# Two adaLN layers on one core: batch 0's feed-forward norm and gate stage put into layer 1's timetable, and weight loads and folds given other times

## The chip, the cores and the metric

One core of a Trainium2 chip runs the whole program. The metric is device microseconds per execution. Engines have their names of the profile: PE is the matmul engine (PEld its weight loads), DVE, ACT and POOL the three others that compute, SP the one that only issues DMAs. POOL issues DMAs too. Each engine works through its own queue in order.

## What is computed

x has 8 batches of 512 tokens by 256 features. Two layers of the same frame follow each other:

```python
def layer(x, c, wmod):
    sa, ca, ga, sb, cb, gb = silu(c) @ wmod          # per batch
    x = x + ga * attention(layernorm(x) * (1 + ca) + sa)
    return x + gb * ffn(layernorm(x) * (1 + cb) + sb)

# layer 1
def attention(h):        # 16 heads of 16, rotary q and k, causal softmax
    q, k, v = rope(h @ wq), rope(h @ wk), h @ wv
    return softmax(causal(q @ k.T / 4)) @ v @ w_proj + b_proj

def ffn(h):              # w1, w2: 256 -> 1024; h1, h2: 1024 -> 1024; w3: 1024 -> 256
    g = silu(h @ w1.T * s1) * (h @ w2.T * s2)
    g = gelu(g @ h1.T * s3)
    g = gelu(g @ h2.T * s4)
    return g @ w3.T * s5
```

Layer 0 has linear attention beside a sliding window of 64, and another feed-forward; the change hardly touches it. The weights w1, w2, h1, h2 and w3 hold -1, 0 and 1.

## The kernel before

**One timetable for three quarters of the work.** All of layer 0 and layer 1's attention are written as small closures, each with a due time, and sorted by it into one order; no scheduler moves them. `when(time, f)` books layer 0, which takes 20 units of time per batch; `when1(time, f)` books layer 1, with 24 units per batch, counted from layer 1's start. Layer 1 starts while the last batch of layer 0 is still at work, so that the two share a stretch (their seam). `in_time` is the one or the other. A closure issues the instructions of one small step (one bank of matmuls, one activation), and each engine's queue is what the sorted order leaves on it.

**Layer 1's attention.** `prepare1(b)` (L939) gets a batch ready. `fetch` loads its rows of `x_mid` (layer 0's result in DRAM). `normed` (L296 and after) books four statistics on DVE (`st`, `mv`), one root on ACT and DVE, and four normalizing activations on ACT. `by_features` transposes the rows on PE, eight 128x128 transposes for a batch, and `modulated` (L993) moves each bank out of PSUM by an ACT activation that applies scale and shift; `hT` is its result. `rotation` makes the q and k of a half of the heads: two matmuls (L1070 among them), an ACT copy (`k`, L1034) and the rotary products on DVE and POOL; the last of its times, in `apart`, are copies. `fold` (L966 to L977) multiplies the projection's weights by the batch's gate row, so that the residual costs nothing later: part 0 fetches the row `bc` on SP, part 1 is two POOL products (L973 the first, into `wps`), parts 2 and 3 two POOL sums. Then, in 6 units for 4 heads, come the scores (L1102, L1160), the exponentials (L1171 on ACT), the causal mask (L1175 on POOL) and the values (L1194). `kept_sums1` (L1204) copies the sums `ys` on ACT, `by_tokens1` (L1210) transposes them, `normalized1` (L1220, L1221) divides on DVE, and `project_out` (L1239 to L1264) transposes into `aT`, projects, and stores to `x_mid`.

**The feed-forward's weights and its flag.** `bring(4)` (L870 to L900), booked at layer 1's unit 48.2, closes layer 0's pools and loads, on SP, the projection's weights `wproj` and `bproj`, and on POOL (L894) w1T, w2T and w3T, 1 MB each. `look` and `low_bits` (L912 to L923) bring every weight once more and reduce its low 12 bits to a column of `low`; `looked` (L928 to L933) reduces `low` to one flag. If no weight has low bits set, products of the weights with a number that is split into two parts, `hi` (cast to fp32r) and `lo` (the rest), are exact enough, and the feed-forward runs in fp32r, two matmuls for each product. Else a plain fp32 version runs. The flag is loaded into a register by all engines (L1451), and a branch follows.

**The feed-forward** (L1321 and after) is ordered by the framework's own scheduler, after the timetable has ended. It opens its own pools, and issues the loads of h1 and h2 on POOL, 512 KB apiece, eight for each (L1337). `layernorm` (L142 to L147) and `transposed` (L157) prepare batch 0. Then for each batch come stage 1 (w1 and w2, `sg` by Silu on ACT L1413, the product `row` on DVE L1414, the two parts by `split` L1341 and L1342), the h1 stage and the h2 stage (L1370 the matmuls, Gelu L1419 and L1425), and w3 with the residual (L1436, L1444, L1445) and the store L1446. Each PSUM bank holds a product of 128 features by 512 tokens; in exact mode `times` makes one by 2 x 2 matmuls in stage 1 (L1370), by 8 x 2 in the h1 and h2 stages.

These two lines of the branch are the seam between timetable and feed-forward:

```python
inexact = nc.values_load(full["flag"][0:1, 0:1], min_val=0, max_val=1)
with tc.If(inexact < 1) as whole:
```

Of the kernel before, what the change touches and what calls it, by code (L numbers as in the profile page):

```python
# [17 lines left out]
P = 128  # L18
# [17 lines left out]
def adaln_two_layers_kernel(ctx: ExitStack, tc: tile.TileContext, t, out):  # L36
# [149 lines left out]
    def mod_rows(pool, b, first, n, bufs=2):  # L186

        bc = pool.tile([P, n, D], FP, name="bc", tag="bc", bufs=bufs)
        nc.sync.dma_start(out=bc, in_=mod_dram[b, first : first + n, :].partition_broadcast(P))
        return bc  # L190

    with ExitStack() as lctx:
# [481 lines left out]
        def finish(b):  # L677
# [45 lines left out]
            for j, ats_ in ((0, (34.6, 34.95)), (2, (35.45, 35.85))):  # L723
# [7 lines left out]
                [t0 + i for i in (35.6, 35.8, 36.28, 36.29)],  # L731
                t0 + 36.5,
                [t0 + 37.4 + 0.15 * j for j in range(NTB)],
                "hr",
# [125 lines left out]
        def bring(i):  # L860
# [7 lines left out]
            elif i == 2:  # L868


                cmask = got1["cmask"] = fm.tile([P, T], FP, name="cmask", tag="cat0", bufs=2)
                nc.gpsimd.memset(cmask, 0.0)
                diag = cmask[:, T - P : T]
                nc.gpsimd.affine_select(
                    out=diag, in_=diag, pattern=[[-1, P]], compare_op=ALU.is_ge, fill=-4e9, base=0, channel_multiplier=1
                )
            elif i == 3:

                home = [rp.tile([P, 2, T], FP, name="home", tag="aw", bufs=4) for _ in range(2)]
                got1["wproj"], wps[0] = (home[0][:, i, :].rearrange("p (k n) -> p k n", k=NC) for i in range(2))  # L880
                got1["bproj"], got1["bc"] = (home[1][:, 0, i * D : (i + 1) * D] for i in range(2))
                nc.sync.dma_start(out=got1["wproj"], in_=w_proj)
                nc.sync.dma_start(out=got1["bproj"], in_=t["L1_attn_b_proj"].partition_broadcast(P))
                nc.sync.dma_start(out=got1["bc"], in_=mod_dram[0, 4, :].partition_broadcast(P))
            else:
                only0.close()
                fpool = ctx.enter_context(tc.tile_pool(name="ffn_w", bufs=1, side="right"))
                lp = got1["lp"] = only1.enter_context(tc.tile_pool(name="only1", bufs=1, side="right"))
                got1["wproj"] = load(lp, "wproj", [P, NC, D], w_proj)
                got1["bproj"] = load(lp, "bproj", [P, D], t["L1_attn_b_proj"].partition_broadcast(P))  # L890

                for name, n, cols in (("w1T", NC, DH), ("w2T", NC, DH), ("w3T", NF, D)):
                    dst = full[name] = fpool.tile([P, n, cols], FR, name=name, tag=name)
                    nc.gpsimd.dma_start(out=dst, in_=t[name].rearrange("(k p) n -> p k n", p=P))  # L894
                for name in ("w1_s_cols", "w2_s_cols", "h1_s_cols", "h2_s_cols"):
                    full[name] = load(fpool, name, [P, NF], t[name])
                full["w3_s"] = load(fpool, "w3_s", [P, D], t["L1_ffn_w3_s"].partition_broadcast(P))
                full["x0"] = fpool.tile([P, NTB, D], FP, name="x0", tag="x0")
                full["low"] = fpool.tile([P, 22], FP, name="low", tag="low")
                full["flag"] = fpool.tile([1, 1], I32, name="flag", tag="flag")  # L900
# [3 lines left out]
        for i, at in enumerate((146.2, 150.0, 157.0, 171.5)):  # L904
            when(at, lambda i=i: bring(i))
        when1(48.2, lambda: bring(4))


# [30 lines left out]
        def prepare1(b):  # L939
# [7 lines left out]

            early = ((135.5, (138.7, 0.3), 139.75, (142.15, 0.4)), (153.0, (160.6, 1.0), 164.6, (165.2, 0.3)))
            usual = (t0 - 37.0, (t0 - 33.6, 1.0), t0 - 29.4, (t0 - 28.6, 0.6))
# [16 lines left out]
            def fold(i):  # L966
                if i == 0:
                    held["bc"] = mod_rows(got1["lp"], b, 4, 1, 1)[:, 0, :] if b else got1["bc"]
                    if b:
                        wps[b] = got1["lp"].tile([P, NC, D], FP, name="wps", tag="wps", bufs=2)  # L970
                elif i == 1:
# [6 lines left out]

            at = (31.0, 49.0)[b] if b < 2 else t0 + 6.5
            for i in range(4):  # L980
                when1(at + (0.0, 3.0, 4.0, 5.0)[i], lambda i=i: fold(i))

# [18 lines left out]
            for c, at in enumerate(((148.38, 149.4), (166.45, 168.9), (t0 - 24.55, t0 - 18.55))[min(b, 2)]):  # L1001
                in_time(at, lambda c=c: by_features(c))
                in_time(at + (0.12 if b == 0 else 0.45), lambda c=c: modulated(c))

# [47 lines left out]
            for c, which, at, begin, then, turn, last in (  # L1052
                (0, "k", -11.55, 152.50, 153.0, (153.3, 153.6, 154.2, 154.8), (156.0, 156.3)),
                (0, "q", -8.55, 153.50, 154.1, (155.0, 155.4, 156.0, 156.6), (157.9, 158.2)),
                (1, "k", 0.45, 156.70, 157.2, (157.5, 158.0, 158.6, 159.2), (160.3, 160.8)),
                (1, "q", 3.45, 157.70, 158.3, (159.9, 160.2, 160.8, 161.4), (162.2, 162.7)),
            ):
# [254 lines left out]
        when1(24 * 3, lambda: nc.gpsimd.dma_start(out=full["x0"], in_=x_mid[0].rearrange("(j p) d -> p j d", p=P)))  # L1312
        when1(24 * B + 2, looked)
        tc.keep_in_program_order(nc.scalar.preload_act_table_set("natural_log_exp_and_others"))
        with tc.manual_schedule():
            for _, _, what in sorted(plan, key=lambda p: p[:2]):
                what()
        only1.close()


    def feed_forward(exact):  # L1321

        with ExitStack() as fctx:
            hp = fctx.enter_context(tc.tile_pool(name=f"hw{exact}", bufs=1 if exact else 3))
            gp = fctx.enter_context(tc.tile_pool(name=f"g2{exact}", bufs=2))
            tok = fctx.enter_context(tc.tile_pool(name=f"tok2{exact}", bufs=1))
            mm = fctx.enter_context(tc.tile_pool(name=f"mm2{exact}", bufs=8, space=PSUM))

            if exact:
                h1 = hp.tile([P, NF, DH], FR, name="h1", tag="h1")
                h2 = hp.tile([P, NF, DH], FR, name="h2", tag="h2")
                for dst, name in ((h1, "h1T"), (h2, "h2T")):
                    src = t[name].rearrange("(k p) n -> p k n", p=P)
                    for k in range(NF):
                        nc.gpsimd.dma_start(out=dst[:, k, :], in_=src[:, k, :])  # L1337
                full.update(h1T=h1, h2T=h2)

            def split(hi, lo, src):  # L1340
                nc.vector.tensor_copy(hi, src)  # L1341
                nc.vector.tensor_tensor(lo, src, hi.bitcast(FP), ALU.subtract)  # L1342

            def halves(name, pool, n):

                if not exact:
                    whole = pool.tile([P, n, T], FP, name=name, tag=name[0])
                    return [whole], lambda k: whole[:, k, :], lambda k: None
                parts = [pool.tile([P, n, T], FR, name=name + e, tag=name[0] + e) for e in "hl"]
                held = {}  # L1350

                def row(k):
                    held[k] = tok.tile([P, T], FP, name="row", tag="row", bufs=3)
                    return held[k]

                return parts, row, lambda k: split(parts[0][:, k, :], parts[1][:, k, :], held.pop(k))

# [20 lines left out]

            if exact:
                w3s = full["w3T"]  # L1380
            else:
                w3s = load(hp, "w3g", [P, NF, D], t["w3T"].rearrange("(k p) n -> p k n", p=P))

            xs, hs = {0: full["x0"]}, {}

            def first_product(b, xn):

                hs[b], row, done = halves("hT", tok, NC)

# [7 lines left out]

            first_product(0, layernorm(tok, xs[0], 1))
            for b in range(B):
                x = xs.pop(b)  # L1400
                if b + 1 < B:
                    xs[b + 1] = tok.tile([P, NTB, D], FP, name="x", tag="x", bufs=2)
                    nc.sync.dma_start(out=xs[b + 1], in_=x_mid[b + 1].rearrange("(j p) d -> p j d", p=P))
                bc = mod_rows(tok, b, 5, 1, 1)
                gb = bc[:, 0, :]
                nc.vector.tensor_tensor(gb, gb, full["w3_s"], ALU.mult)  # L1406
                h = hs.pop(b)
                g1, row, done = halves("g1", gp, NF)
                for f in range(NF):
                    pa = times("w1T", NC, f * P, h)  # L1410
# [4 lines left out]
                    done(f)  # L1415
                g2, row, done = halves("g2", gp, NF)
                for f in range(NF):
                    ps = times("h1T", NF, f * P, g1)
                    nc.scalar.activation(row(f), ps, AF.Gelu, scale=full["h1_s_cols"][:, f : f + 1])  # L1419
                    done(f)  # L1420
                xn = layernorm(tok, xs[b + 1], 1) if b + 1 < B else None
                g3, row, done = halves("g3", gp, NF)
                for f in range(NF):
# [7 lines left out]
                for j in range(0, NTB, 2):  # L1431
                    ps = mm.tile([P, 2, D], FP, name="mm", tag="mm")
                    for i in range(2):
                        for k in range(NF):
                            for m, part in enumerate(g3):
# [6 lines left out]
                                )  # L1442
                    tmp = tok.tile([P, 2, D], FP, name="tmp", tag="row", bufs=3)
                    nc.vector.tensor_tensor(tmp, ps, bcast(gb, [P, 2, D], 1), ALU.mult)  # L1444
# [3 lines left out]
                        in_=tmp,  # L1448
                    )

    inexact = nc.values_load(full["flag"][0:1, 0:1], min_val=0, max_val=1)  # L1451
# [72 lines left out]
```

## Time and profile before

| | |
|---|---|
| median of 3 runs | 1852.07 us (1851.04 to 1859.65) |
| the profiled execution | 1848.55 us |
| its span in the trace | 1846.8 us |
| its mean granted PE clock | 0.982 |
| feed-forward's first PE work to the end | 1178.2 to 1846.8 us |

The page has busy times of each engine over the span, 40 slices of the span with a busy digit each (9 is 90% or more) and the clock granted to PE in tenths, queues, a chain that ended last, and groups of instructions. The timeline lists instructions in order of their start: start, duration, engine, line of the kernel, operation, output <- inputs, shape, and in brackets how long the engine had idled before it and what ended that. The waits are listed as engine, line, what released it, and then the total idle time, the count, and the longest. An answer by windows gives for each stretch its length, then busy time and count of PE, PEld, DVE, ACT and POOL, and last the granted clock, the share of DMA busy and its GB/s.

### The profile page before, as it was taken

To read this page: it belongs to the slowest core of one execution; us is meant where nothing else is said; L and a number is where in the kernel's file an instruction comes from. 1 tells how busy PE (TensorE), PEld (TensorE's weight loads), DVE (VectorE), ACT (ScalarE), POOL (GpSimd) and SP (SyncE) were. 2 spreads that over 40 slices of the span, in tenths; PEclk is the share of its full clock that TensorE was granted. 3 is DMA by queue.
4 is the path that set the end of the run, shared out by engine and by line. 5 is a ranking of instruction groups with operands and counts; after the bars stand their busy time and mean duration, and the time that the engine had idled before them with its cause. 6 is when DMAs were issued, how large, how long until landed. Compare 5 with 4: busy or idle time off the path is not lost. (4 is left out here: it accounts for less than half of the span.)

```text
span 1846.8 us, 41143 instructions
## 1 busy us (share of the span) xinstructions
PE 1753.8 (95%) x16878; PEld 1193.4 (65%) x16878; DVE 1075.9 (58%) x3717; ACT 887.2 (48%) x1274; POOL 716.4 (39%) x1094
## 2 busy tenths in 40 slices
PE   3999999999999989989999999799999999999998
PEld 2456566665666655545455455588888888888887
DVE  3555665756656555568888877546353544636353
ACT  1676766767667645556666655422121322212221
POOL 4566857668575663456656554200000000000000
PEclk7999999999999999999999999899999999999999
DMA  4100001010001101042121110600000000000000
GB/s 149 45 2 14 20 25 36 5 36 17 28 16 33 40 4 38 7 123 70 52 72 52 60 60 25 220 1 15 1 26 7 21 26 1 26 1 26 1 15 14
DMA packets 41893, 65.98 MB, mean 36 GB/s; under 512 B 4056, under 2 KB 33368, under 8 KB 41696
## 3 DMA queue, kind: packets, MB, share of 16 engines
q1 hardware_dynamic: 36512, 47.02, 8.1%
q0 software_dynamic: 5184, 16.25, 2.8%
q8 instruction: 134, 2.20, 0.5%
q14 instruction: 63, 0.52, 0.1%
HBM read 50.63 MB, written 12.63 MB: 34 GB/s over the span
## 5 line engine op out<-in xcount | busy, mean ns | idle before, releaser
L1113 DVE CUSTOM_DVE_ANT_0 junk<-sc,cmask 128x256 bf16<-128x256 f32 (+3 forms) x512 | 225.2, 487 | 102.7 <-PE sc L1102 102.1
L1171 ACT ACTIVATE at<-sc 128x768 f32<-128x768 f32 (+1 forms) x192 | 168.6, 881 | 118.1 <-PE sc L1102 103.6
L571 POOL TENSOR_SCALAR_AFFINE_SELECT aw<-aw 64x512 f32<-64x512 f32 (+1 forms) x320 | 167.6, 550 | 99.5 <-ACT aw L561 93.5
L1370 PE MATMUL mm<-g2h,h 128*128 128x512 f32 x512 | 199.9, 390 | 0.0
L1370 PE MATMUL mm<-g2l,h 128*128 128x512 f32 x512 | 199.2, 389 | 0.0
L1370 PE MATMUL mm<-g1l,h 128*128 128x512 f32 x512 | 198.7, 390 | 0.0
L1370 PE MATMUL mm<-g1h,h 128*128 128x512 f32 x512 | 198.0, 390 | 0.0
L1102 PE MATMUL sc<-k,q 32*128 32x512 f32 (+3 forms) x1024 | 191.7, 471 | 4.9 <-ACT at L1171 4.9
L485 ACT ACTIVATE at<-sc 128x768 f32<-128x768 f32 (+1 forms) x192 | 164.0, 883 | 64.2 <-PE sc L474 63.5
L1160 PE MATMUL sc<-qs,k 32*128 32x384 f32 (+3 forms) x1024 | 189.1, 469 | 0.8 <-DVE qs L1144 0.8
L1175 POOL TENSOR_SCALAR_AFFINE_SELECT at<-at 128x256 f32<-128x256 f32 x256 | 101.6, 409 | 189.3 <-ACT at L1171 189.0
L518 DVE CUSTOM_DVE_ANT_0 junk<-sc,wmask 128x128 bf16<-128x128 f32 x512 | 115.2, 285 | 79.8 <-PE sc L507 79.6
L489 POOL TENSOR_SCALAR_AFFINE_SELECT at<-at 128x256 f32<-128x256 f32 x256 | 103.4, 425 | 103.5 <-ACT at L485 99.4
L1425 ACT ACTIVATE row<-mm,h_s_cols 128x512 f32<-128x512 f32 x64 | 44.0, 688 | 194.1 <-PE mm L1370 194.1
L1160 PEld LDWEIGHTS sc<-qs,k 32*128 32x128 f32 x1024 | 81.5, 184 | 67.6 <-DVE maxima L1113 37.2
L1419 ACT ACTIVATE row<-mm,h_s_cols 128x512 f32<-128x512 f32 x64 | 43.9, 687 | 158.1 <-PE mm L1370 158.1
L1370 PEld LDWEIGHTS mm<-g1l,h 128*128 128x128 f32 x512 | 96.1, 188 | 22.3 <-DVE g1l L1342 2.3
L1370 PEld LDWEIGHTS mm<-g1h,h 128*128 128x128 f32 x512 | 95.8, 188 | 20.4 <-DVE g1h L1341 0.5
L1370 PEld LDWEIGHTS mm<-g2h,h 128*128 128x128 f32 x512 | 96.1, 188 | 19.8
L1370 PEld LDWEIGHTS mm<-g2l,h 128*128 128x128 f32 x512 | 96.1, 188 | 19.7
L1341 DVE CAST g2h<-row 128x512 fp32r<-128x512 f32 x64 | 27.3, 427 | 133.2 <-ACT row L1419 133.2
L1413 ACT ACTIVATE sg<-mm,w_s_cols 128x512 f32<-128x512 f32 x64 | 44.0, 688 | 121.4 <-PE mm L1370 60.8
(223 smaller groups left out, 3951.4 us busy)
## 6 DMA issues: line engine op xcount, KB each, us to landing
x_mid<-x SPq DMA_DIRECT2D x16, 512.0 KB, 3.2
x<-x_mid POOLq DMA_DIRECT2D x9, 512.0 KB, 4.3
x<-in_L_attn_x_dram SPq DMA_DIRECT2D x8, 512.0 KB, 4.4
raw<-in_h1T_dram SPq DMA_DIRECT2D x8, 512.0 KB, 3.4
raw<-in_h2T_dram SPq DMA_DIRECT2D x8, 512.0 KB, 3.4
h<-in_h1T_dram POOLq DMA_DIRECT2D x8, 512.0 KB, 8.0
h<-in_h2T_dram POOLq DMA_DIRECT2D x8, 512.0 KB, 10.0
out_dram<-tmp SPq DMA_DIRECT2D x16, 256.0 KB, 2.6
```

What stands on the lines that cost most here:

```text
L485: nc.scalar.activation(at, ps[:, :, :o], AF.Square, scale=0.5)
L489: nc.gpsimd.affine_select(out=d, in_=d, pattern=[[0, 2], [1, P]], compare_op=ALU.is_ge, fill=0.0, base=0, channel_multiplier=-1,)
L518: nc.vector.tensor_tensor_reduce(junk, ps[:, i, ii * P : (ii + 1) * P], wmask[:, int(blk > 0), :], -1.0, BIG, ALU.add, ALU.min, maxima[:, ...
L571: nc.gpsimd.affine_select(out=d, in_=d, pattern=[[0, d.shape[1]], [sign, 64]], compare_op=ALU.is_ge, fill=0.0, base=0, channel_multiplier= ...
L1102: nc.tensor.matmul(ps[:, i, o : o + m], q[r, e, qb * P : (qb + 1) * P], k[r, e, :m], start=True, stop=True,)
L1113: nc.vector.tensor_tensor_reduce(junk[:, :m], ps[:, i, o : o + m], got1["cmask"][:, T - m :], -1.0, BIG, ALU.add, ALU.min, maxima[:, NTB * ...
L1160: nc.tensor.matmul(ps[:, i, o : o + m], k[r, e, kb * P : (kb + 1) * P], qs[r, kb * P : T], start=True, stop=True)
L1171: nc.scalar.activation(at, ps[:, :, :o], AF.Exp, scale=0.25)
L1175: nc.gpsimd.affine_select(out=d, in_=d, pattern=[[0, 2], [1, P]], compare_op=ALU.is_ge, fill=0.0, base=0, channel_multiplier=-1,)
L1370: nc.tensor.matmul(ps, w[:, k, col : col + P], part[:, k, :], start=(k == 0 and i == 0), stop=(k == n - 1 and i == len(parts) - 1),)
L1413: nc.scalar.activation(sg, pa, AF.Silu, scale=full["w1_s_cols"][:, f : f + 1])
L1425: nc.scalar.activation(row(f), ps, AF.Gelu, scale=full["h2_s_cols"][:, f : f + 1])
```

## The change

**Weights.** w1T and w2T are loaded at units 62.9 and 68.9 of layer 1, no longer with `bring(4)` at 48.2. w3T is loaded by the feed-forward itself, on POOL behind h2. The folds' products `wps` lie in another pool.

**Folds and times.** Batch 1's fold has its parts at 49, 55, 57 and 59 (before 49, 52, 53 and 54); batch 2's begins at 61 (before 54.5). Batch 1's statistics and root, in the seam of the two layers, are booked earlier, `modulated` of batch 2 a quarter unit earlier, the `apart` copies of batch 0's second half and one norm of layer 0's batch 7 later. The flag's reduction comes at unit 184 (before 194).

**Batch 0 of the feed-forward.** Its norm, its transposes, `modulated8` and `split` are booked in the timetable where a ninth batch's would lie (units 158.4 to 175.4). At 187, `room` closes layer 1's pool and places the two parts of `g`, stage 1's result. `gated(f)` makes the two products of a 128-feature group into one of the three PSUM banks of the scores, 8 matmuls; `gate_parts` is the Silu on ACT, the product and the two parts on DVE. The eight groups are booked at units 200 to 216, among the last values, transposes and projections of batch 7. The feed-forward's batch 0 begins with the h1 stage.

**Pools of the feed-forward.** h2, w3, the second `g` and the token buffers are placed first and h1 last, so h1 lies higher, over layer 1's `aT`. `g` alternates between two fixed pairs, the `row` buffers are 6 (before 3), `sg` and `bc` 2 (before 1).

```diff
-                t0 + 36.5,
-                [t0 + 37.4 + 0.15 * j for j in range(NTB)],
+                t0 + (36.5 if b < B - 1 else 37.0),
+                [t0 + (37.4 if b < B - 1 else 37.6) + 0.15 * j for j in range(NTB)],
...
-                for name, n, cols in (("w1T", NC, DH), ("w2T", NC, DH), ("w3T", NF, D)):
-                    dst = full[name] = fpool.tile([P, n, cols], FR, name=name, tag=name)
-                    nc.gpsimd.dma_start(out=dst, in_=t[name].rearrange("(k p) n -> p k n", p=P))
+                for name in ("w1T", "w2T"):
+                    full[name] = fpool.tile([P, NC, DH], FR, name=name, tag=name)
...
+                full["h"] = [fpool.tile([P, NC, T], FR, name="h" + e, tag="h" + e) for e in "hl"]
...
+        for i, name in enumerate(("w1T", "w2T")):
+            when1(
+                62.9 + 6 * i,
+                lambda name=name: nc.gpsimd.dma_start(out=full[name], in_=t[name].rearrange("(k p) n -> p k n", p=P)),
+            )
...
-            early = ((135.5, (138.7, 0.3), 139.75, (142.15, 0.4)), (153.0, (160.6, 1.0), 164.6, (165.2, 0.3)))
+            early = ((135.5, (138.7, 0.3), 139.75, (142.15, 0.4)), (153.0, (160.2, 0.3), 162.0, (165.2, 0.3)))
...
-            at = (31.0, 49.0)[b] if b < 2 else t0 + 6.5
+            at = (31.0, 49.0, 61.0)[b] if b < 3 else t0 + 6.5
             for i in range(4):
-                when1(at + (0.0, 3.0, 4.0, 5.0)[i], lambda i=i: fold(i))
+                when1(at + (0.0, 6.0, 8.0, 10.0)[i] if b == 1 else at + (0.0, 3.0, 4.0, 5.0)[i], lambda i=i: fold(i))
...
-                (1, "k", 0.45, 156.70, 157.2, (157.5, 158.0, 158.6, 159.2), (160.3, 160.8)),
-                (1, "q", 3.45, 157.70, 158.3, (159.9, 160.2, 160.8, 161.4), (162.2, 162.7)),
+                (1, "k", 0.45, 156.70, 157.2, (157.5, 158.0, 158.6, 159.2), (161.3, 162.3)),
+                (1, "q", 3.45, 157.70, 158.3, (159.9, 160.2, 160.8, 161.4), (163.3, 164.3)),
...
-        when1(24 * B + 2, looked)
+        when1(184.0, looked)
+
+        def room():
+            only1.close()
+            gpool = ctx.enter_context(tc.tile_pool(name="ffn_g", bufs=1, side="right"))
+            full["g"] = [gpool.tile([P, NF, T], FR, name="g" + e, tag="g" + e) for e in "hl"]
+
+        t0 = 24 * B
+        ln8 = normed(when1, lambda: full["x0"], [t0 - 33.6 + j for j in range(NTB)],
+                     t0 - 29.4, [t0 - 28.6 + 0.6 * j for j in range(NTB)], "h")
...
+        for c in range(NC):
+            when1(t0 - 24.55 + 6 * c, lambda c=c: by_features8(c))
+            when1(t0 - 24.1 + 6 * c, lambda c=c: modulated8(c))
+            when1(t0 - 22.6 + 6 * c, lambda c=c: parts8(c))
+
+        def gated(f):
+            ps = held8[f] = sc.tile([P, 2, T], FP, name="sc", tag="sc")
+            for i, name in enumerate(("w1T", "w2T")):
+                for k in range(NC):
+                    for m, part in enumerate(full["h"]):
+                        nc.tensor.matmul(
+                            ps[:, i, :],
+                            full[name][:, k, f * P : (f + 1) * P],
+                            part[:, k, :],
+                            start=(k == 0 and m == 0),
+                            stop=(k == NC - 1 and m == 1),
+                        )
+
+        def gate_parts(f, i):
+            ps = held8[f]
+            if i == 0:
+                held8["sg", f] = tok.tile([P, T], FP, name="sg", tag="rot")
+                nc.scalar.activation(held8["sg", f], ps[:, 0, :], AF.Silu, scale=full["w1_s_cols"][:, f : f + 1])
+            else:
+                row = tok.tile([P, T], FP, name="row", tag="flat", bufs=2)
+                nc.vector.scalar_tensor_tensor(
+                    row, ps[:, 1, :], full["w2_s_cols"][:, f : f + 1], held8.pop(("sg", f)), ALU.mult, ALU.mult
+                )
+                split([part[:, f, :] for part in full["g"]], row)
+
+        when1(187.0, room)
+        for f, at in enumerate((200.0, 200.6, 203.7, 209.6, 211.0, 214.0, 215.0, 216.0)):
+            when1(at, lambda f=f: gated(f))
+            for i in range(2):
+                when1(at + (0.3, 0.35)[i], lambda f=f, i=i: gate_parts(f, i))
...
-        only1.close()
...
-            first_product(0, layernorm(tok, xs[0], 1))
+            hs = {0: full["h"]}
+            x = full["x0"]
+            if not exact:
+                first_product(0, layernorm(tok, x, 1))
...
-                for f in range(NF):
+                for f in range(0 if b or not exact else NF, NF):
```

## The prediction, made before the changed kernel ran

> **What bounds the kernel now.** First the page's busy shares and its 40 slices.
>
> ```profile
> PE 1753.8 (95%) x16878; PEld 1193.4 (65%) x16878; DVE 1075.9 (58%) x3717; ACT 887.2 (48%) x1274; POOL 716.4 (39%) x1094
> ...
> PE   3999999999999989989999999799999999999998
> ...
> PEclk7999999999999999999999999899999999999999
> ```
>
> TensorE (PE) is full but for 93 us; nothing on other engines counts unless it opens a hole in PE. So I read next who PE waited for, then the two slices with a 7 and an 8 in time order.
>
> ```profile
> PE mm L1070 <- ACT hT L993: 7.9, 5, 5.7
> ...
> PE mm L157 <- DVE xn L147: 7.0, 1, 7.0
> ```
>
> The 7.0 us hole is the seam between layer 1's attention and the feed-forward. Its timeline:
>
> ```profile
> 1161.99 2.36 PE L1194 MATMUL mm<-at,vo 128*32 128x512 f32 x32 [2.01 <-POOL at L1175]
> ...
> 1164.42 0.58 ACT L1204 COPY ys<-mm 128x512 f32<-128x512 f32 x1 [2.96 <-PE mm L1194]
> ...
> 1175.91 4.50 POOL L1337 DMA_DIRECT2D h<-in_h1T_dram  x8 [13.98 <-DMA x_mid<-x]
> ...
> 1178.21 2.10 PE L157 MATMUL mm<-ident,xn 128*128 128x128 f32 x8 [7.00 <-DVE xn L147]
> ...
> 1181.65 0.79 PE L1370 MATMUL mm<-hTh,w1T 128*128 128x512 f32 x1 [1.34 <-DVE hTh L1341]
> 1181.68 0.53 POOL L1337 DMA_DIRECT2D h<-in_h2T_dram  x1 [1.27 <-DMA h<-in_h1T_dram]
> 1182.96 0.53 POOL L1337 DMA_DIRECT2D h<-in_h2T_dram  x1 [0.74 <-DMA h<-in_h1T_dram]
> ...
> 1199.30 0.40 PE L1370 MATMUL mm<-g1h,h 128*128 128x512 f32 x1
> ```
>
> PE ends the projection of batch 7 at 1171.2, norms and transposes batch 0 until 1181.65, and does the first gate stage (64 matmuls) until 1199.30, where the h1 stage begins. From there PE never waits long: in the chain of waits the batches end 82 us apart. So **1199.30** is the number that the change must move. Granted clock by stretches:
>
> ```profile
> 726.60:730.10 3.50, 3.50 (x20) 0.79 (x20) 2.03 (x9) 3.23 (x7) 1.74 (x3) 0.51 0.02 5
> ...
> 1160.00:1171.20 11.20, 7.95 (x60) 5.04 (x60) 1.37 (x3) 3.19 (x5) 1.16 (x3) 1.00 0.01 2
> 1171.20:1178.20 7.00, 0.00 (x1) 0.02 (x1) 3.71 (x14) 1.58 (x2) 2.29 (x5) 0.68 0.75 202
> 1173.80:1187.40 13.60, 7.85 (x22) 5.97 (x23) 8.93 (x33) 3.47 (x4) 7.14 (x13) 0.50 1.08 353
> ```
>
> After the hole the clock is at half until 1187.4, so the gate stage cost 17.65 us where 64 x 0.23 (spacing at full clock, 1199.30 to 1199.53) is 14.7.
>
> The other hole, inside layer 1:
>
> ```profile
> 824.86 1.26 POOL L973 TENSOR_TENSOR wps<-wproj,bc 128x512 f32<-128x512 f32 x1 [3.40 <-DMA raw<-in_w1T_dram]
> ...
> 830.43 2.07 PE L1070 MATMUL mm<-wqkv,hT 128*128 128x256 f32 x4 [5.67 <-ACT hT L993]
> ```
>
> POOL's fold for batch 1 waits behind 3 MB of feed-forward weights; ACT's `k` (L1034) waits 5.38 for the rotation queued behind the fold, L993 stands behind ACT, and PE lacks a PSUM bank. The same L1070 wait starts at 888.73, 944.54, 1000.37 and 1056.19: 55.8 us a batch, but 58.3 after this hole (half clock 829.0 to 835.9).
>
> **Part 1, weights loaded later, fold of batch 1 later.** w1T and w2T go from unit 48.2 to 62.9 and 68.9, w3T out of the layer; the fold's multiply goes from unit 52 to 55 (a unit is 55.8/24 = 2.33 us). The wproj load then has no 3 MB beside it and 7 us more. Gain: 5.67 + (58.3 - 55.8) = **8.2**. POOL's order changes: two folds (2 x 4.5 us: 1.27 + 0.72 + 2 x 1.27) lie among rotations, but POOL works only 33.4 of 55.8 us in a batch, so I cost the move at nothing; without that cover a fold's 4.5 us holds ACT as above. Each 1 MB issue holds POOL 0.73. The `bc` fetch of batch 2 goes on SP from unit 54.5 to 61 and must land by 64; it took 3.3 us, there are 7. If w1T beside it delays it by the same 3.4 us it still lands; if not, 4 of the 8.2 come back. Range 4 to 8.2.
>
> **Part 2, batch 0's norm inside layer 1.** Added about units 158 to 174: DVE 4 statistics (0.41 + 0.18), a root chain (1.0), two splits (0.43 + 0.69 each), 5.6 us; ACT 4 x 0.6 + 2 x 0.77 + 0.5, 4.4 us; PE 8 transposes of 4 to a bank, 2 x 0.53 = 1.1. They take the places a batch 8 would have, and there a batch fills DVE 44.9 and ACT 34.0 of 55.8 us, so only PE's 1.1 counts, plus 0.5 where PE now waits for the flag's reduction at unit 184 (PE was full there; at 194 it was not), plus 0.4 for queueing: **+2.0**, range +1 to +5. The flag itself is early.
>
> **Part 3, gate stage in the tail.** The eight gates (8 matmuls, 1.85 us each) stand in PE's order between layer 1's last steps. By rows: g0 1159.9 to 1161.8, in the 2.01 hole ahead of L1194, free. Values end 1164.3, g1 1166.15. New wait: ACT's copy of ys (1164.42 before) now stands behind a table load (1.28) and two Silu (0.69), the second of which needs all of g1: it ends 1167.65, and PE idles 1.05. Then transposes to 1168.2, g2 1170.05, transposes 1170.5, g3 1172.4, projection 0.94, g4 1175.2, two projections 1177.1, g5 1178.95, the last projection **1179.9**, g6, g7 to **1183.65**. DVE needs 1.86 a gate (1194.74 to 1196.59 in the gate stage of before), PE 1.85, so three score banks suffice; if DVE lagged it would cost up to 2.
>
> **Part 4, h1's weights.** In the changed program h1 is the first POOL load after the branch, and its first chunk lies on the place of `aT`, read last by the projection that ends at 1179.9. It used to wait for the x_mid store (13.98 us, to 1175.91). So this transfer starts 4 us later than before: what was cover is now the bound. From 1180.1 the first chunk lands after 5.5 us (issue 1175.91, first landing about 1181.4, released L1337 again), the others 1.28 apart: 1185.6 to 1194.6. PE's new order runs 3, 4, 6, 7, 7, 7, 7 matmuls on chunks 0 to 6, 41 before chunk 7 is asked for. They end at 1196.1, as if a dense h1 stage had begun at 1196.1 - 41 x 0.23 = **1186.6**. Gain 1199.3 - 1186.6 = **12.7**; range 8 (landing as slow as the median 8.0 us of the h1 issues, and 2 for DVE) to 15.3 (no load wait, PE from 1184, its branch included). h2 and w3, behind h1 on POOL, are needed 29 us later.
>
> The Trainium skill speaks on this: DMA: Bandwidth & Descriptors, section Anatomy of one DMA, fits 2.0 us plus bytes over 436 GB/s for a POOL-issued load, 3.2 us for 512 KB. By it PE would start 2.3 us earlier; the trace's 5.5, with other loads beside it, is what I use.
>
> **Clock.** Between g7 and the first chunks PE has holes of 2.0, 0.6 and 0.4. At 726.6 the clock halved for 3.5 us after holes of under 1 us; from 1160 to 1171, 71% busy, it stayed full. I take one half spell on busy PE: **+1.7**, range 0 to +5.
>
> Against this stands the Trainium skill, TensorE: Matmul & The Clock Gate, section Why this matters for your kernels: without an idle gap over about 3 us there is no drop. The rows at 726.6 disagree. By the rule the sum is 1.7 lower.
>
> **Part 5, seam of layers 0 and 1.** Batch 1's statistics and root come 2.6 units earlier, batch 7's norm and the `apart` copies of batch 0 later. Here ACT waited 3.39 for `mv`, PE 0.97 + 0.77 + 1.0 + 0.62, and the clock halved twice (2 x 1.7). Bounds: all 6 gone; or ACT waits elsewhere, +3. I take **-1.0**: the holes are ACT's queue, which keeps its work.
>
> **Sum.** 1848.55 - 8.2 + 2.0 - 12.7 + 1.7 - 1.0 = 1830.4 for a profiled execution (span 1846.8). The median of the runs shown is 1852.07, 3.5 above it: I carry three quarters of it over (2.6) and say **1833**. Steady feed-forward batches keep PE's order almost unchanged: nothing there.
>
> **Rivals.** *Only the tail pays* (0.08): the fold, or the two 1 MB loads, make the hole at L1070 again; the 8.2 go: 1841. For: POOL's queue is in order. Against: 3.4 us wait against 7 us of room. *Nothing moves* (0.11): h1 lands slowly and the clock halves in the tail, so h1 starts near 1195, and parts 2 and 5 cost 5 + 3: 1833 + 8.4 + 3 + 4 + 3.3, 1852. *Slower* (0.07): the clock halves at the first gates and stays there, since the tail's PE work is broken by ACT and DVE replies. PE has 8 x 1.85 + 7.6 = 22 us of work there, which doubles, and some 10 us of h1 at half add 5 more: 1833 - 1.7 + 27 = 1858 and, with the projection and so h1's load late by its share (8), 1866. It decides once PE is idle in each 3.5 us stretch from 1162 on, as at 726.6; against it, 1160 to 1171 kept 1.00 with more idle than the new tail has. *More* (0.06): seam 0/1 also clears, 1825.
>
> **Chances.** Forecast 0.68, 1825 to 1841. A measurement tells about 0.5% (9.3 us): faster by more 0.81 (the forecast, More, and most of Only the tail), within 0.12, slower 0.07. The range: every term at its good end gives 1848.55 - 8.2 + 1 - 15.3 - 6 = 1820.0, at its bad end 1848.55 - 4 + 5 - 8 + 5 + 3 = 1849.6; both extremes together are unlikely, so I stop short of the bad end, past Only the tail: 1821 to 1847.
>
> **To look for.** Right: no wait over 1 us at L1070 near 830; the first h matmul of the h1 stage 10 to 15 us earlier against the layer; POOL's first h1 issue released by L1262 on PE, not by x_mid; ACT ys late by 3. Wrong: PEclk at 0.5 in the tail; a new wait of PE on DVE between gates; POOL waits above 1 us at the fold.

## The result, and the profile after

The changed kernel takes **1849.08 us** (median of 13 runs, 1845.47 to 1851.61), the kernel before 1854.43 (median of 13, 1849.38 to 1859.65). The ratio is 0.9973, 95% interval 0.9963 to 0.9983: 5 us faster where 19 were forecast (1852.07 to 1833), and 2 us outside the range. The profiled execution of the changed kernel took 1849.27 us (span 1847.6).

The page after, the PE parts:

```profile
PE 1764.1 (95%) x16878; PEld 1193.8 (65%) x16878; DVE 1077.0 (58%) x3715; ACT 887.2 (48%) x1278; POOL 717.3 (39%) x1094
...
PE   3999999999999989999999999899999999999998
...
PEclk7999999999999999999999999999999999999999
```

Both dips that the prediction read are shallower: the 8 in slice 18 is a 9, the 7 in slice 26 an 8. But PE is busy 10.3 us longer (1753.8 before) with the same 16878 matmuls. Holes were closed, and matmuls became slower. The waits of PE, from the list of the changed kernel:

```profile
PE mm L1262 <- ACT aT L1252: 4.1, 6, 2.3
...
PE mm L1080 <- ACT hT L1003: 2.8, 5, 0.6
...
PE mm L1459 <- DVE row L1387: 1.8, 1, 1.8
...
PE mm L1459 <- DMA h<-in_h1T_dram: 1.6, 2, 1.1
```

L1080 is L1070 of before: its longest wait is 0.6 (5.7 before). The 7.0 us hole at the norm is gone. New are a wait of 2.3 us at the projection (L1262) and small ones where the h1 stage (now L1459) begins.

**Where the time went.** Each PE instruction has its partner in the other trace, so the difference of their starts, read at a few places, is a ledger. The kernel before was traced twice, since its first trace (1848.55 us) turned out 6 us under its median; the second execution took 1857.0 us.

| stretch (us in the first trace of before) | after minus first trace | after minus second trace |
|---|---|---|
| layer 0, to 629 | +4.9 | +0.1 |
| seam of the layers, to 816 | +0.8 | -0.5 |
| fold of batch 1, to 851 | -6.7 | -6.0 |
| fold of batch 2, to 879 | +4.0 | +4.0 |
| rest of layer 1, to 1154 | +0.8 | +0.7 |
| tail and start of the h1 stage, to 1230 | -10.2 | -12.6 |
| feed-forward to the end | +6.9 | +6.4 |
| sum | +0.5 | -7.9 |

The medians differ by 5.35, between the two columns. The 4.9 us in layer 0, which the change hardly touches, are the clock. One stretch from the first trace of before and the same from the changed kernel (length, busy time and count of five engines, granted clock, DMA share, GB/s):

```profile
99.40:102.80 3.40, 3.40 (x42) 1.26 (x30) 1.29 (x14) 2.34 (x4) 2.34 (x6) 1.00 0.00 0
```

```profile
99.40:102.80 3.40, 3.40 (x54) 1.31 (x43) 1.78 (x16) 2.35 (x4) 1.39 (x4) 0.50 0.00 0
```

The second trace of before also has half the clock there, and at 61.8 and 143.7, as the changed kernel's trace has; against it 0.1 us is left of the 4.9. Such spells come in some executions and not in others. The second trace has one more in the tail (granted clock 0.50 from 1167.7 to 1171.1), which lies in its -12.6; the first trace has none there and is the cleaner partner for the tail.

What has to be explained is the +4.0 and the +6.9, which took back over 10 of some 17 to 19 us.

**The new wait at 861.** From the timeline of the changed kernel:

```profile
855.00 1.27 POOL L1037 TENSOR_TENSOR flat<-flat,rope 128x512 f32<-128x512 f32 x1
856.23 1.26 POOL L983 TENSOR_TENSOR wps<-wproj,bc 128x512 f32<-128x512 f32 x1
857.57 0.74 POOL L984 TENSOR_TENSOR bc<-bc,bproj 128x256 f32<-128x256 f32 x1
858.26 0.77 POOL L1185 TENSOR_SCALAR_AFFINE_SELECT at<-at 128x256 f32<-128x256 f32 x2
858.99 1.27 POOL L1037 TENSOR_TENSOR flat<-flat,rot 128x512 f32<-128x512 f32 x1
...
860.29 0.81 ACT L1044 ACTIVATE k<-flat,hot,half 128x512 f32<-128x512 f32 x1 [2.20 <-POOL flat L1037]
...
861.01 0.56 ACT L1252 COPY aT<-mm 128x512 f32<-128x512 f32 x1
...
861.63 1.13 PE L1262 MATMUL mm<-wps,aT 128*128 128x256 f32 x4 [2.29 <-ACT aT L1252]
```

The two products of batch 2's fold (L983, L984) stand between the second and the third product of a rotation (L1037). ACT's `k` waits 2.20 for that, the `aT` copy stands behind `k`, and PE waits 2.29 for `aT`. It is the kind of chain that made the old hole at 830, one batch later and with another copy behind `k`.

**The slower matmuls.** The groups of the h1 and h2 stages on the pages, two of before and then those of the changed kernel (count, busy time, mean ns of one):

```profile
L1370 PE MATMUL mm<-g1l,h 128*128 128x512 f32 x512 | 198.7, 390 | 0.0
L1370 PE MATMUL mm<-g1h,h 128*128 128x512 f32 x512 | 198.0, 390 | 0.0
```

```profile
L1459 PE MATMUL mm<-gh,h 128*128 128x512 f32 x1024 | 402.9, 395 | 3.5 <-DVE row L1387 1.8
L1459 PE MATMUL mm<-gl,h 128*128 128x512 f32 x1024 | 401.5, 394 | 0.0
```

Same shape, same clock, 5 ns more each: 2048 x 5 ns is 10 us. (By busy time, with 199.9 and 199.2 us for the two groups of g2 before, it is 8.6 of PE's 10.3 us.) By starts, a matmul follows the other in 227 ns in the h1 and h2 stages of before (medians); after, in 227 only in the h2 stages of even batches, and on average in 232.4 to 233.4 in the others. The +6.9 is a net: before, about half of the h1 stages also have up to five steps of 0.27 to 0.45 us, up to 0.7 us a stage, which the changed kernel no longer has from batch 1 on. What made them stays open. The pairs of `g` alternate, so odd and even batches differ in where their operands lie, and in nothing else that PE sees.

### The profile page after: what moved, and what is told of

The parts are those of the page before. It is cut to its first block, busy times and chain, and to the rows that moved or that the text cites. A ratio compares the mean times of both kernels' runs of the same rounds, so it can differ in the third digit from the quotient of the medians.

```text
span 1847.6 us, 41122 instructions
## 1 busy us (share of the span) xinstructions
PE 1764.1 (95%) x16878; PEld 1193.8 (65%) x16878; DVE 1077.0 (58%) x3715; ACT 887.2 (48%) x1278; POOL 717.3 (39%) x1094
## 4 chain that ended last, share of the span: by engine, by line
PE 81%; ACT 8%; POOL 5%; DVE 3%; issue 2%; DMA 1%; POOLq 0%; SPq 0%; ACTq 0%
PE mm L1459 31%; PE sc L1170 7%; PE mm L716 5%; PE mm L165 4%; PE mm L619 4%; PE sc L479 4%; PE mm L1204 3%; PE mm L1522 3%; PE mm L1022 3%; PE sc L556 2%; PE mm L1262 2%; ACT at L490 2%; PE mm L1080 2%; PE mm L642 2%; PE mm L444 2%
## 5 line engine op out<-in xcount | busy, mean ns | idle before, releaser
L1459 PE MATMUL mm<-gh,h 128*128 128x512 f32 x1024 | 402.9, 395 | 3.5 <-DVE row L1387 1.8
L1459 PE MATMUL mm<-gl,h 128*128 128x512 f32 x1024 | 401.5, 394 | 0.0
L194 DVE CAST gh<-row 128x512 fp32r<-128x512 f32 x192 | 80.9, 425 | 258.1 <-ACT row L1505 131.6
L1459 PEld LDWEIGHTS mm<-gh,h 128*128 128x128 f32 x1024 | 192.5, 188 | 50.2 <-DMA h<-in_h1T_dram 3.9
L1459 PEld LDWEIGHTS mm<-gl,h 128*128 128x128 f32 x1024 | 192.3, 188 | 44.4
L523 DVE CUSTOM_DVE_ANT_0 junk<-sc,wmask 128x128 bf16<-128x128 f32 x512 | 115.3, 285 | 81.9 <-PE sc L512 81.7
L195 DVE TENSOR_TENSOR gl<-row,gh 128x512 fp32r<-128x512 f32 x192 | 131.6, 689 | 7.5
L479 PE MATMUL sc<-qm,qk 32*128 32x512 f32 (+3 forms) x1024 | 101.3, 474 | 1.1 <-ACT at L490 0.6
L1112 PEld LDWEIGHTS sc<-k,q 32*128 32x128 f32 x1024 | 82.8, 185 | 13.2 <-ACT at L1181 8.9
L1499 ACT ACTIVATE sg<-mm,w_s_cols 128x512 f32<-128x512 f32 x56 | 38.6, 690 | 105.7 <-PE mm L1459 102.1
L566 ACT ACTIVATE aw<-sc 128x1024 f32<-128x1024 f32 (+1 forms) x64 | 62.2, 972 | 48.2 <-PE sc L556 44.0
```

Source lines behind the costliest of these rows:

```text
L195: nc.vector.tensor_tensor(parts[1], src, parts[0].bitcast(FP), ALU.subtract)
L479: lambda i=i, r=r, kb=kb, n=n, o=o: nc.tensor.matmul(ps[:, i, o : o + n], k[r, e, kb * P : (kb + 1) * P], qm[r, e, kb * P : T], start=True ...
L523: nc.vector.tensor_tensor_reduce(junk, ps[:, i, ii * P : (ii + 1) * P], wmask[:, int(blk > 0), :], -1.0, BIG, ALU.add, ALU.min, maxima[:, ...
L1112: nc.tensor.matmul(ps[:, i, o : o + m], q[r, e, qb * P : (qb + 1) * P], k[r, e, :m], start=True, stop=True,)
L1459: nc.tensor.matmul(ps, w[:, k, col : col + P], part[:, k, :], start=(k == 0 and i == 0), stop=(k == n - 1 and i == len(parts) - 1),)
```

## The experiments

**The kernel before once more.**

> The kernel before once more, for a second trace. Theory: its h1 and h2 stages step at 227 ns in all batches again, and its layer 0 takes 4 to 5 us more than in the first trace, as the changed kernel's does, because that part of the first trace was a lucky one (1848.55 against a median of 1854.43). Rival: layer 0 is as short as in the first trace, and the changed kernel itself lost the 5 us there.

1857.0 us. Its h1 and h2 stages step at 227 ns again, and up to 629 it lies 4.8 us behind the first trace. So the first trace was a lucky one, and the prediction, which summed from it, started 6 us too low (it added 2.6 for that).

**Does the place of the operands set the pace?** Groups of 64 matmuls with given addresses, alone on the chip:

```python
cells = [..., (17536, 83072, 115840, 0), ..., (17536, 58496, 74880, 0), (118272, 58496, 74880, 0), ...]
for w, hi, lo, g in cells:          # weights, the two moving parts, where the split goes
    ...                             # 4 x 8 x 2 matmuls as in the h1 stage
```

> This kernel leaves out the whole network: it fills 175 KB of each partition with ternary weights and then runs 37 groups of 64 matmuls of 128x128 by 128x512 in fp32r, built like the h1 stage, each group with its weights and its moving operand at given addresses; groups 30 to 35 add the Gelu and the split of the feed-forward, the others run with no other engine at work. In the traces the h1 and h2 stages of the kernel before step at 227 ns a matmul, in the changed kernel at 232 to 235 ns where the weights lie at 118272 or the moving operand at 162528, at 227 ns where both lie below 91264. Theory placement: the group with 17536 and 83072 steps at 227 ns, those with 118272 or 162528 at 232 or more with no other engine working, and the scan of small offsets and of high places that keep the remainder of the address by 4096 tells whether it is the remainder or the height. Rival traffic: without other engines all groups step at 227 ns, and only groups 32 to 35 separate.

With no other engine at work 17536 with 83072 steps at 226.7, 118272 with 58496 at 232.4, 17536 with 162528 at 233.6. So traffic is not the cause. Height is not either: 160896, 148608 and 115840, which all leave 128 by 256, step at 226.7. Moving one operand of a good pair by 32, 64, 96 or 128 bytes makes it 229 to 234; by 256 it is 227 again. With Gelu and split beside them the same placements step at 226.7 and at 233.3 to 234.5.

> The network is left out again: 24 groups of 64 matmuls, no other engine at work. In the first such run a group stepped at 227 ns when the addresses of weights and moving operand both left 128 after division by 256 (at any height), at 229 to 234 ns in the others, but no group had another remainder equal on both sides. Theory absolute: only 128 is fast, groups with equal remainders of 0, 32, 64, 96, 160, 192 or 224 step at 232 to 235. Rival congruent: they step at 227 like 128, since only the difference counts. Further groups take plain fp32 (four passes, some 900 ns) and 256 columns: if the cost is per read of an operand, fp32 with a remainder of 0 loses 4 x 5 ns a matmul, and 256 columns lose 5 of 120 ns.

The rival held. From the groups of this run (four tiles a placement, one shown of each: remainders 0 and 0, 224 and 224, then 0 and 128, 128 and 0):

```profile
L91 PE MATMUL c__244<-big 128*128 128x512 f32 x16 | 3.8, 389 | 0.0
...
L91 PE MATMUL c__720<-big 128*128 128x512 f32 x16 | 3.8, 390 | 0.0
...
L91 PE MATMUL c__788<-big 128*128 128x512 f32 x16 | 3.9, 394 | 0.0
...
L91 PE MATMUL c__856<-big 128*128 128x512 f32 x16 | 3.9, 394 | 0.0
```

All eight equal remainders step at 226.7 to 227.1, the unequal ones at 232.4. A group in which only one of the two moving parts lies 128 off steps at 230.0, about halfway. Only the difference counts: **weights and moving operand must be congruent by 256 bytes**. Plain fp32 does not care (two records of 429.1 or 429.2 ns a matmul in all five placements), and with 256 columns nothing is lost (117 to 120 ns whichever).

**The same in the kernel.** Three tiles that nobody uses:

```diff
+                fpool.tile([P, 32], FP, name="pad0", tag="pad0")       # before the two parts "h"
+                fpool.tile([P, 56], FP, name="pad1", tag="pad1")       # at the end of that pool
+                hp.tile([P, 32], FP, name="pad2", tag="pad2")          # before h1
```

> The changed kernel with three unused tiles of 128, 224 and 128 bytes, which give every operand of the feed-forward's matmuls an address with remainder 128 by 256; nothing else differs. Theory placement: all h1 stages 28.8 us (29.6 in the changed kernel), odd h2 stages 29.7 (30.5), stage 1 14.3 (14.7), so 8 x 0.8 + 4 x 0.8 + 7 x 0.4 = 12 us less over the feed-forward: near 1837, and 81.2 us a batch. Rival: stage 1 and the rest are slow by the DVE and ACT work beside them, and the time stays at 1849.

1836.68 us, ratio to before 0.9895 (0.9861 to 0.9929). (By the order and sizes of the tiles stage 1's weights and `h` both lie at remainder 224 here, the rest at 128: equal, though not all 128.) Its groups:

```profile
L1462 PE MATMUL mm<-gh,h 128*128 128x512 f32 x1024 | 398.6, 390 | 3.9 <-DVE row L1389 1.9
L1462 PE MATMUL mm<-gl,h 128*128 128x512 f32 x1024 | 396.7, 389 | 0.0
```

The stages of batches 1 to 6 (counted from 0), by starts of PE:

| us | stage 1 | h1 | h2 | batch |
|---|---|---|---|---|
| before | 14.9 | 29.1 to 29.6 | 29.9 | 81.9 to 82.5 |
| after | 14.9 | 29.7 to 29.9 | 29.9 (even), 30.7 (odd) | 82.6 to 83.5 |
| after with pads | 14.5 | 29.0 | 29.9 | 81.5 |

Stage 1 was slow in both kernels (weights at remainder 224, `h` at 0 before and at 96 after): 0.4 us a batch that the kernel before also lost. So the pads gain more than the change of pools had cost: from the first h2 stage's start to PE's last matmul it is 611.8 us before, 618.8 after and 607.5 with pads.

**And in the kernel before, the other way round**: h1 alone 32 bytes higher.

> The kernel before with h1 alone 32 bytes higher, so that its address is not congruent by 256 with that of g; h2 and everything else keep their remainders. Theory placement: each h1 stage steps at 232 to 234 ns and takes 29.5 to 29.7 us (28.8 before), the h2 stages stay at 29.7, and the whole loses 8 x 0.8 = 6.4 us. Rival: one operand's remainder matters only in the changed kernel's pools; the stage stays at 28.8.

1864.13 us, in one run, where seven runs of the kernel before beside it have a median of 1857.08. Its groups:

```profile
L1372 PE MATMUL mm<-g1l,h 128*128 128x512 f32 x512 | 202.1, 397 | 0.1
L1372 PE MATMUL mm<-g1h,h 128*128 128x512 f32 x512 | 200.9, 396 | 0.0
L1372 PE MATMUL mm<-g2h,h 128*128 128x512 f32 x512 | 199.9, 390 | 0.0
L1372 PE MATMUL mm<-g2l,h 128*128 128x512 f32 x512 | 199.3, 389 | 0.0
```

g1 (the h1 stage) is slow, g2 is not. The h1 stages take 29.9 to 30.5 us where both traces of before have 29.1 to 29.7: 0.8 more, 6.4 in eight batches.

**The fold of batch 2 in a pause of the rotations.**

```diff
-                when1(at + (0.0, 6.0, 8.0, 10.0)[i] if b == 1 else at + (0.0, 3.0, 4.0, 5.0)[i], lambda i=i: fold(i))
+                when1(at + ((0.0, 3.0, 4.0, 5.0), (0.0, 6.0, 8.0, 10.0), (0.0, 7.2, 8.2, 9.2))[b if b in (1, 2) else 0][i], lambda i=i: fold(i))
```

> The changed kernel with the fold of batch 2 later: its products at unit 68.2, its sums at 69.2 and 70.2, in a pause of the rotations, not at 64 to 66 among them. Theory fold: the 2.3 us wait of PE for the aT copy at 861 and the loss after it are the fold on POOL ahead of a rotation product; both go, 3.5 to 4 us less against the layer at unit 72, near 1845. Rival: the wait comes from the w1T load or from ACT's own queue and stays; same time as the changed kernel, 1849.

1845.15 us (ratio to before 0.9944, 0.9924 to 0.9964). Between 850 and 882 it gains 4.0 us on the changed kernel, and nothing else in layer 1 moves. The wait in its list, 2.3 at the longest before:

```profile
PE mm L1262 <- ACT aT L1252: 2.2, 6, 0.4
```

**The two halves of the hole at 830**, both on the kernel before. First only the weights later (w1T, w2T, w3T at units 62.9, 68.9, 74.9), then only the folds of the last run, the weights at 48.2 as ever.

> The kernel before with w1T, w2T and w3T loaded at units 62.9, 68.9 and 74.9, the folds where they were. Theory loads: the 5.7 us hole at L1070 near 830 came from the wproj load behind 3 MB, so it goes with the loads alone, 6 to 8 us less against the layer. Rival position: the fold itself, 4.5 us of POOL among the rotation products, makes a hole of 2 to 4 us there also without the loads, as the one of batch 2 did at 861 in the changed kernel.

> The kernel before with the fold's times of the last repair alone (batch 1 at 49, 55, 57, 59, batch 2 at 61, 68.2, 69.2, 70.2), w1T, w2T and w3T still loaded at 48.2. Theory both: moving the loads alone left a wait of 2.25 us at L1070 (5.67 before), so the place of the fold and the loads each made a part of it; with the fold out of the rotations the loads delay nobody, the wait falls to the 0.56 of every other batch, and 6 to 8 us go. Rival loads: 3 MB beside the rotations' and norms' traffic still hold something up, 3 us or more remain near 830.

The loads alone: the hole falls from 5.67 to 2.25, and 5.1 us go against the first trace of before, 4.5 against the second. The folds alone: 0.56 is left, and 6.7 and 6.1 us go, as much as both together in the changed kernel. The lists:

```profile
PE mm L1074 <- ACT hT L997: 4.5, 5, 2.2
```

```profile
PE mm L1070 <- ACT hT L993: 2.8, 5, 0.6
```

So a fold among the rotations makes a hole of 2 us even when its data is there (1.6 us of time here, 4.0 at 861), and with the fold in a pause the loads need not move at all for the time's sake. (One run each, 1852.44 and 1848.29 us.)

**Both repairs, and what bounds h1.** Pads and later fold together:

> The changed kernel with both repairs, the three pads and the later fold of batch 2. The two act in different stages, so they should add: 1836.7 less 4.0, 1832.7. Rival: the saved wait at 861 comes back before the tail (for instance as a wait for the flag or for h1), 1836.

1835.7 us (1832.53 to 1836.49), ratio 0.9890 (0.9865 to 0.9915). The 4.0 us at 861 are there in its trace, but two half-clock spells (1154.0 and 1188.1) give back 1.6, and four runs do not tell 1835.7 from 1836.68: the sum is not shown in the time.

> The kernel with both repairs, and h1's chunk 0, the only one that lies over aT, loaded last; the products with h1 take chunk 0 last as well, in all batches. Theory load: what bounds the start of the h1 stage is h1's load, which stands behind the last read of aT; chunks 1 to 7 can then be issued some 15 us earlier, right after the last values, and the dense h1 stage begins 3 to 4 us sooner: 1829. POOL's first h1 issue is then at about 1168 and not 1184. Rival splits: DVE's last split of the gates ends at about 1190 and bounds it just as well, under 1.5 us.

> The kernel with both repairs, and h1 3328 bytes higher, so that it no longer lies over aT (its address keeps the remainder 128). In the run with chunk 0 last, POOL's first h1 issue stayed at 1180.8: the first load of the tile waits for everything that lay under any part of h1, and the last of that is the projection's read of aT. Theory load: without aT under it the first issue follows the last values, near 1168, h1 is there before the gates end, PE's wait for an h1 chunk goes, and the dense h1 stage begins 2 to 3 us sooner than in the version with both repairs. Rival splits: PE waits as long for DVE's last splits instead, under 1 us.

Both missed: 1832.98 and 1834.57 us, not told apart from 1835.7, and POOL's first h1 load waits as before (1180.78 and 1181.04). Where aT is taken out from under h1, the queue's wait is still for the projection's last matmul: POOL's wait for PE ends at 1180.11, 0.04 us after it, and 0.03 to 0.04 us after it with aT underneath. So a tile's first use waited for more than lay in its own place. Whether the closed pool under it counts as a whole, or all that lies under its own pool, these runs do not tell apart. The next version avoids both by a pool of its own:

```diff
+                hp2 = fctx.enter_context(tc.tile_pool(name="hw2", bufs=1))
+                h1 = [(hp if k < 2 else hp2).tile([P, DH], FR, name=f"h1k{k}", tag=f"h1k{k}") for k in range(NF)]
...
+                    for k in [*range(2, NF), 0, 1] if name == "h1T" else range(NF):
```

> Both repairs, and h1 in eight tiles: chunks 2 to 7 in a pool of their own above all that the projection reads, loaded first and multiplied first; chunks 0 and 1, which lie lower, come last. In the run with h1 moved up as a whole the first issue stayed at 1181.0; the wait in the queue is still the projection's last read of aT, which holds back the whole pool. Here the first load waits for the last values alone. Theory load: POOL's first h1 issue comes near 1168, six chunks are there before the gates end, PE's wait of 1.0 us for an h1 chunk near 1196 goes and so does the interleaved, broken start; the h1 stage of batch 0 takes 29.5 us or less (32.3 to 32.7 in the other versions), 3 us less: 1831 to 1832. Rival splits: DVE's last split holds PE just as long; the stage keeps 31.5 us or more and the time stays within 1.5 us of 1834.6.

The issues of h1 on POOL, from the timeline of the run before this one and of this one:

```profile
1181.04 4.31 POOL L1425 DMA_DIRECT2D h<-in_h1T_dram  x8 [18.65 <-DVE row L1389]
```

```profile
1167.43 3.26 POOL L1426 DMA_DIRECT2D h1k<-in_h1T_dram  x6 [3.31 <-DVE gh L194]
1182.33 1.23 POOL L1426 DMA_DIRECT2D h1k<-in_h1T_dram  x2 [11.64 <-ACT sg L1386]
```

Six chunks are asked for 13.6 us earlier; the two in the lower pool, which by the tiles' sizes do not lie over aT either, still wait for the projection. No wait of PE for an h1 chunk is left (a hole of 1.75 us ahead of the first stays); batch 0's h1 stage takes 29.1 us (32.95 in the changed kernel), and its end comes 3.5 us earlier against the layer than in the run before. This version takes **1830.66 us** (1826.95 to 1832.65), ratio 0.9862 (0.9842 to 0.9882), the lowest median of all; by the times alone, four runs each, it is not told apart from the two versions before it.

## Why the prediction was wrong, step by step

- **Part 1** (8.2 forecast, range 4 to 8.2; measured 6.0 to 6.7, then 4.0 given back, so 2 to 2.7). The gain came, within its range, though 8.2 counted the whole hole of 5.67 while the same wait is 0.56 in every other batch. The step that failed is "POOL works only 33.4 of 55.8 us in a batch, so I cost the move at nothing". An average share of POOL says nothing of the place: the rotations are runs of three products that ACT waits for, and the fold fell into one. The price named for lost cover, "a fold's 4.5 us holds ACT", is near the 4.0 that came.
- **Part 2** (+2.0; measured +0.7 to +0.8 up to 1154): right in kind, below its range of +1 to +5.
- **Parts 3 and 4 with the clock** (-12.7 + 1.7 = -11.0; measured -10.2 and -12.6): right in kind, since its steps came in the order it gave, but that -11.0 lies so near is in part luck. The half spell did not come, and without it -10.2 by the first trace stands against -12.7. The rows (h1 issue and matmul starts) are:

```profile
1184.45 4.32 POOL L1422 DMA_DIRECT2D h<-in_h1T_dram  x8 [18.68 <-DVE row L1387]
...
1189.02 0.47 PE L1459 MATMUL mm<-gh,h 128*128 128x512 f32 x1 [1.82 <-DVE row L1387]
...
1191.64 0.50 PE L1459 MATMUL mm<-gh,h 128*128 128x512 f32 x1 [0.54 <-DMA h<-in_h1T_dram]
...
1199.83 0.50 PE L1459 MATMUL mm<-gh,h 128*128 128x512 f32 x1 [1.07 <-DMA h<-in_h1T_dram]
```

  The changed kernel is 3.8 us late here against the first trace. Less that, the h1 issue comes at 1180.6 (forecast 1180.1). The last chunk is there at 1196.0 by the same reckoning (forecast 1194.6). PE had done 34 matmuls when it waited for it, not 41; 1199.83 - 34 x 0.232 - 3.8 is 1188.1, as if dense from there (forecast 1186.6). The rest of the shortfall is the slower pace and small holes. DVE's product for the last gate (L1387) holds the first matmul for 1.82, within the 2 that the text allowed for DVE. The bracket's name for POOL's wait, a DVE row, is the event that came last by the profile; the queue waits for the projection, as the runs with h1 elsewhere showed.
- **Clock** (+1.7): 0 in the changed kernel's trace, but two of the seven traces with the new tail have a half spell as the h1 stage begins. From the version with both repairs, the stretch ahead of it and the spell:

```profile
1171.00:1188.10 17.10, 15.23 (x69) 12.09 (x68) 12.79 (x21) 4.60 (x7) 4.32 (x8) 1.00 0.28 84
1188.10:1191.60 3.50, 3.45 (x9) 2.24 (x8) 0.00 (x0) 0.00 (x0) 0.00 (x0) 0.51 1.10 385
```

  PE was busy 15.2 of the 17.1 us ahead of it, with no hole over 1.9. The Trainium skill (TensorE: Matmul & The Clock Gate, section Part 1: The HAM clock gate) lets the clock fall after an idle window of about 3.4 us; this row shows a fall without such a window, as the one at 726.6 in the prediction did.
- **Part 5** (-1.0): +0.8 and -0.5. The two traces of before differ by 1.3 in this stretch, so nothing can be said.
- **"Steady feed-forward batches keep PE's order almost unchanged: nothing there"** is the step that cost most: a term put at nothing, measured at +6.4 to +6.9. PE's order was no cause: the pads alone, with the order as it was, took it back. What the pools moved was the operands' addresses, and the kernel before had its h1, h2 and g congruent by 256. A sign stood in the first trace: stage 1 stepped at 234 ns (remainders 224 and 0), the h1 stage at 227, same shape and same clock. The prediction took 0.23 for both and did not ask why they differ.
- **The start of the sum**: 1848.55 was 5.9 us under the median of 13 runs; 2.6 were added.

None of the rivals was it. "Nothing moves" named the time nearly (1852), by a slow h1 load and a halved clock, and neither came. "Only the tail pays" had the fold hold up PE again: half of that came, at the projection and not at L1070.

Together: -2.7 (fold) + 0.8 + 0.8 - 10.2 + 6.9 = -4.4 by the first trace, without layer 0's clock, against 5.35 between the medians. The forecast had -18.2: of the 13.8 missing, 6.9 are the addresses and 5.5 the fold. With 3.3 for the start of the sum that is, to about 1 us, the 16 by which 1833 was missed.

## What to carry to other kernels

A change that moves pools moves addresses: look whether the mean ns of a matmul group of the same shape changes on the page, and in fp32r with 512 columns place weights and moving operands at the same remainder by 256 bytes; three pads of 128, 224 and 128 bytes were worth 12 us here, more than the rearranged stage. A short job moved in a queue is free only in a gap of that queue, not because the engine's share is low: read the queue's rows at the new place. In these runs a first load into reused memory waited for more than the last reader of its own place, so early loads want a pool of their own, clear of what is read late.

## What the runs showed of the hardware

- fp32r matmuls of 128x128 by 128x512 in a row start 226.7 to 227.4 ns apart when the addresses of weights and moving operand are congruent by 256, and 229.1 to 234.5 ns apart when they are not, at all heights tried and with or without work on ACT and DVE. The loss is not the same for all differences (229.1 with the moving operand 64 higher, 232.4 to 233.3 with 128). Plain fp32 and 256 columns show no loss. Why 256 counts was not found.
- Half-clock spells of 3.4 to 7 us in the first 150 us come and go between executions of the same work: two traces of the kernel before differ by 4.8 us at 629 by them.
